# Four slots from the small table instead of three in a mixture-of-experts stage

## The chip, the core and the metric

The program runs on one NeuronCore of a Trainium2 chip, as one launch. Its engines run side by side, each on its own list of instructions: PE (TensorE, matrix products), DVE (VectorE), ACT (ScalarE), POOL (GpSimd) and SP (SyncE, which here only issues transfers). A transfer issued on SP's queue or POOL's queue is carried out by the core's 16 DMA engines. The metric is the time of one execution in microseconds (us). Three runs of the kernel before took 600.97, 602.80 and 606.39 us; the median is 602.8 us.

## What is computed

The input is `x`, 8 batches of 512 tokens of 256 numbers. A first half (an adaptive layer norm, a projection, a short convolution, a 16-state scan and a projection back) is added to `x` under a gate per batch. The second half is a mixture of eight experts, of which each token uses the best one:

```python
h = _layernorm(x, axis=-1) * (1 + cb) + sb
x = x + gb * _L0_ffn_ref(h, ...)

logits = x @ wr + br                      # 8 experts
top_p, top_i = top_k(softmax(logits), 2)
gate = top_p[:, 0] / (top_p[:, 0] + top_p[:, 1])
for e in range(8):                        # only where top_i[:, 0] == e
    hmid = gelu(x @ w1[e] + b1[e])        # 256 -> 1024
    hout = hmid @ w2[e] + b2[e]           # 1024 -> 256
    out += where(top1 == e, hout * gate, 0)
```

All numbers are 32-bit floats. How many tokens an expert gets is known only when the program runs.

## The kernel before, in words

**Stage one** goes through the eight batches. For every token it writes a row of 1028 numbers (4112 bytes) to `xp_d` in DRAM: the result of the first half, its norm and gate, and the batch's three modulation vectors. The token's number is scattered into `ids_d`, a list in DRAM with a region per expert, by four transfers of POOL's queue per batch (`ids_d<-tok,row`).

**Stage two** works in slots. A slot is up to 256 tokens of one expert. It needs the numbers of its tokens (`name_tokens`, line 1023: SP loads a register from a table, then issues `ids<-ids_d`, 1 KB), its expert's weights (`expert_of`, line 1035: SP loads a register, then issues `w1t`, 1 MB, line 1041; `b1t`, line 1044; `b2t`, line 1045; and `w2t`, 1 MB, line 1048), and the rows of its tokens (`rows_of`, line 1055: two transfers of POOL's queue of 128 rows each, `xg<-xp_d,ids`). DVE makes `hg` from `xg`, PE transposes it (`tp<-ident,hg`) and multiplies it with `w1t` (`layer1`, line 1083: eight blocks `ph`, 32 matmuls); ACT applies gelu; PE multiplies with `w2t` (`layer2`, line 1259: two blocks `py`, 32 matmuls); DVE finishes, and POOL scatters the rows to the output (`out<-ot,ids`).

Which expert and which tokens a slot has comes from one of two tables. The **small table** (`early_table`, line 958) is made after six of the eight batches: it holds the first `NEARLY` full groups of 256 tokens. Their rows may be gathered before stage one ends. The **late table** is made after the last batch, and its slots can be named only when the last four `ids_d` scatters have landed. It has `NPAIR = 16 - NEARLY` slots of two tiles and seven of one tile, of which four are always worked on; the other three stand behind a branch (line 1323) that the profiled execution did not take. So 20 slots are worked on: `NEARLY` early ones, then the late ones in the order that lines 1249 to 1255 write out.

```python
got = [slot0, fetched(1, pre[1])] + [fetched(i) for i in range(2, NEARLY)]   # line 1165
...
name_tokens(slots[NEARLY])                                                   # line 1317
work(slots, got, (slot0, gl0, hTs[1]))
```

`fetched` (line 1150) asks for a slot's weights and, unless they are given, its rows. `work` (line 1289) names and fetches slots ahead of the one at hand. Slots 0 and 1 get their rows in stage one (`pre`), slot 0 its weights and first layer too. The weights of the other slots go round four buffers (`wts`), their rows round five.

**The order** in which instructions stand on each engine is not the order in which they are written. All of this is recorded, and a planner (`Plan.order`, line 191) sorts it: it gives each operation an estimated length, takes the operation that can start first by its own clock, and among equals the one that is due first. It counts the transfers of one stage as one wire at 300 GB/s. What it puts out is fixed; on the chip each engine then runs its list in order, and an instruction that waits holds up all that stand behind it. That holds for SP too, whose list is register loads and transfers. The compiled program gives the transfers of SP eight completion lanes in turn, and a transfer waits until the one eight places before it has landed.

Below, slots are called 0, 1, 2 and so on in the order of work; slot 3 is the first late slot before the change, slot 4 after it.

Of the kernel before, what the change touches and what calls it, by code (L numbers as in the profile page):

```python
# [10 lines left out]
FP = mybir.dt.float32  # L11
# [7 lines left out]
P = 128  # L19
# [270 lines left out]
def adaln_mamba_moe_kernel(  # L290
# [16 lines left out]
    B, L, D = x.shape  # L307
# [6 lines left out]
    KF = FF // P  # L314
# [4 lines left out]
    JB = BLK // P  # L319


    FEW, NEARLY = 6, 3
    assert (FEW * NT - E) // 2 + 1 >= NEARLY


# [91 lines left out]
    ids = epool.tile([P, NEARLY + NSLOT, JB], I32, name="ids")  # L417
# [13 lines left out]
    with tc.tile_pool(name="wa", bufs=1) as wa, tc.tile_pool(  # L431
        name="a3", bufs=3
    ) as a3, tc.tile_pool(
        name="a2", bufs=2
    ) as a2, tc.tile_pool(
        name="rowp", bufs=2
    ) as rowp, tc.tile_pool(
        name="sm", bufs=4
    ) as sm, tc.tile_pool(name="ps_t", bufs=2, space=PSUM) as ps_t, tc.tile_pool(
        name="ps_x", bufs=3, space=PSUM  # L440
    ) as ps_x, tc.tile_pool(name="ps_s", bufs=1, space=PSUM) as ps_s, tc.tile_pool(
        name="ps_o", bufs=2, space=PSUM
# [570 lines left out]
        def tiles(i):  # L1013
            return JB if i < NEARLY + NPAIR else 1

        def loads(fn, outs, ins, length):

            if nc is plan:
                plan.call("sync", fn, outs, ins, length)
            else:  # L1020
                fn()

        def name_tokens(i):
            jb, at_ = tiles(i), where[i][1]

            def fn():
                o = chip.sync.value_load(at_, min_val=0, max_val=E * TOK)  # L1027
                chip.sync.dma_start(  # L1028
                    out=ids[:, i, 0:jb],
                    in_=ids_d[bass.ds(o, jb * P), :].rearrange("(p j) o -> p (j o)", j=jb),  # L1030
                )

            loads(fn, [ids[:, i, 0:jb]], [at_, *id_views[: FEW * NT]], 0.8)

        def expert_of(i, w1t, w2t, b1t, b2t, behind=()):

            number = where[i][0]

            def fn():
                e = chip.sync.value_load(number, min_val=0, max_val=E - 1)  # L1040
                chip.sync.dma_start(  # L1041
                    out=w1t, in_=w1[bass.ds(e, 1)].rearrange("o (k p) f -> p (o k) f", p=P)
                )
                chip.sync.dma_start(out=b1t, in_=par[:, bass.ds(e * KF, KF)])
                chip.sync.dma_start(
                    out=b2t, in_=b2[bass.ds(e, 1)].rearrange("o d -> (o d)").partition_broadcast(P)
                )
                chip.sync.dma_start(
                    out=w2t, in_=w2[bass.ds(e, 1)].rearrange("o (k p) d -> p (o k) d", p=P)
                )  # L1050

            loads(fn, [w1t, b1t, b2t, w2t], [number, *behind], 2.5)
            return i, w1t, b1t, b2t, w2t

        def rows_of(i, xg, upto):

            for j in range(tiles(i)):
                nc.gpsimd.indirect_dma_start(
                    out=xg[:, j, :], out_offset=None, in_=xp_d[0:upto, :],
                    in_offset=bass.IndirectOffsetOnAxis(ap=ids[:, i, j : j + 1], axis=0),  # L1060
                    bounds_check=upto - 1, oob_is_err=False,
                )
            return xg
# [19 lines left out]
        def layer1(t, hT, gl, ph_tile):  # L1083
            i, w1t, b1t, b2t, w2t, xg = t
            n = tiles(i) * P
            for f in range(KF):
                ph = ph_tile()
                for k in range(KD):
                    nc.tensor.matmul(
                        ph[:, 0:n], lhsT=w1t[:, k, f * P : (f + 1) * P], rhs=hT[:, k, 0:n],  # L1090
                        start=(k == 0), stop=(k == KD - 1),
                    )
                nc.scalar.activation(gl[:, f, 0:n], ph[:, 0:n], AF.Gelu, bias=b1t[:, f : f + 1])
            return gl
# [4 lines left out]
        for b in range(B):  # L1099
# [6 lines left out]
            if b == FEW - 1:  # L1106
# [5 lines left out]
                pre, hTs = [], []  # L1112
                for i in range(2):
# [13 lines left out]
                slot0 = (*expert_of(  # L1127
                    0, *weights, epool.tile([P, KF], FP, name="b1_0"),
                    epool.tile([P, D], FP, name="b2_0"), pre,
                ), pre[0])  # L1130
# [7 lines left out]
    with tc.tile_pool(name="g", bufs=2) as gp, tc.tile_pool(  # L1138
        name="wts", bufs=4
    ) as wts, tc.tile_pool(name="tab", bufs=1) as tab, tc.tile_pool(  # L1140
        name="blk", bufs=6
    ) as blk, tc.tile_pool(name="blk2", bufs=2) as blk2, tc.tile_pool(name="ps_r", bufs=2, space=PSUM) as ps_r, tc.tile_pool(
        name="ps_h", bufs=4, space=PSUM
# [3 lines left out]
        nc.due = behind + 4 * SLOT  # L1147
        turn = count_from()

        def fetched(i, xg=None):  # L1150
            t = expert_of(
                i, wts.tile([P, KD, FF], FP, name="w1t"), wts.tile([P, KF, D], FP, name="w2t"),
                blk.tile([P, KF], FP, name="b1t"), blk.tile([P, D], FP, name="b2t"),
            )
            if xg is None:

                at = next(turn) % 5
                pool, n = (blk, 3) if at < 3 else (blk2, 2)
                xg = rows_of(
                    i, pool.tile([P, JB, ROW], FP, name="xg", tag=f"xg_{n}", bufs=n),  # L1160
                    FEW * L if i < NEARLY else TOK + BLK,
                )
            return (*t, xg)

        got = [slot0, fetched(1, pre[1])] + [fetched(i) for i in range(2, NEARLY)]


        half = tab.tile([1, 2 * E], I32, name="half")
# [90 lines left out]
        def layer2(t, gl):  # L1259

            i, w1t, b1t, b2t, w2t, xg = t
            mg = xg[:, :, OWN:ROW]
            ot = gp.tile([P, JB, D], FP, name="ot")
            for j in range(tiles(i)):
                py = ps_y.tile([P, D], FP, name="py")
                for f in range(KF):
                    nc.tensor.matmul(
                        py, lhsT=gl[:, f, j * P : (j + 1) * P], rhs=w2t[:, f, :],
                        start=(f == 0), stop=(f == KF - 1),
                    )  # L1270
                nc.vector.tensor_tensor(ot[:, j, :], py, b2t, ALU.add)
                nc.vector.tensor_tensor(ot[:, j, :], ot[:, j, :], mg[:, j, 2 * D : 3 * D], ALU.mult)
                nc.vector.scalar_tensor_tensor(
                    ot[:, j, :], ot[:, j, :], xg[:, j, D + 2 : D + 3], xg[:, j, 0:D],
                    ALU.mult, ALU.add,
                )
                nc.gpsimd.indirect_dma_start(
                    out=outf[i * JB + j],
                    out_offset=bass.IndirectOffsetOnAxis(ap=ids[:, i, j : j + 1], axis=0),
                    in_=ot[:, j, :], in_offset=None, bounds_check=TOK - 1, oob_is_err=False,  # L1280
                )

        def made(t):
            return features(
                t[0], t[-1], gp.tile([P, JB, D], FP, name="hg"),
                gp.tile([P, KD, BLK], FP, name="hT"), ps_r.tile([P, KD, BLK], FP, name="tp"),
            )

        def work(slots, got, begun=None):


            ahead, pending = len(got), None
            hT = None if begun else made(got[0])
            for n in range(len(slots)):
                nc.due = behind + (n + 1) * SLOT
                if n + ahead + 1 < len(slots):
                    name_tokens(slots[n + ahead + 1])
                if n + ahead < len(slots):
                    got.append(fetched(slots[n + ahead]))
                if n == 0 and begun:  # L1300
                    nxt = begun[2]
                else:
                    nxt = made(got[n + 1]) if n + 1 < len(slots) else None
                if n == 0 and begun:
                    layer2(*begun[:2])
                else:
                    gl = layer1(
                        got[n], hT, gp.tile([P, KF, BLK], FP, name="gl"),
                        lambda: ps_h.tile([P, BLK], FP, name="ph"),
                    )  # L1310
                    if pending is not None:
                        layer2(*pending)
                    pending = (got[n], gl)
                hT = nxt
            layer2(*pending)

        name_tokens(slots[NEARLY])
        work(slots, got, (slot0, gl0, hTs[1]))
        plan.emit()
        nc = chip  # L1320
        more = nc.values_load(filled[0:1, 0:1], min_val=0, max_val=NSING)
        for at, part in ((FIRST, rest[:1]), (FIRST + 1, rest[1:])):
            with tc.If(more > at):
                for i in part:
                    name_tokens(i)
                work(part, [fetched(i) for i in part])
# [56 lines left out]
```

## Time and profile before

| what | value |
|---|---|
| median of three runs | 602.8 us (600.97 to 606.39) |
| the profiled execution | 602.82 us, of which 601.0 us from the first to the last instruction (the span) |
| mean granted PE clock | 0.968 of full speed |
| PE busy | 563.9 us, 94% of the span, 2882 matmuls |
| DVE, ACT, POOL busy | 58%, 35%, 35% |
| DMA | 96.73 MB, mean 161 GB/s |
| stage two on PE | from about 321 us (`py` of slot 0) to 587 us |

Times inside the execution are counted in us from its first instruction. In a row of the timeline the columns are the start, the duration, the engine and the source line, the operation with its output and inputs, the number of instructions merged into the row, and in brackets how long the engine was idle before, and what ended it. Most operations are issued through one recording helper, so that nearly all rows name lines 154 and 159; the tile names tell them apart. In a row of a stretch the columns are its bounds, its length, the busy time of each engine with the number of its instructions, the granted PE clock, the busy share of the DMA engines, and what they moved. A chain row is a piece of the chain of work that ended last: start, duration, what. "SPq" is SP's queue of transfers: there the duration of a row includes the time in which the transfer could not be issued.

### The profile page before, as it was taken

How to read it: one execution, taken by the hardware profiler on the slowest of the kernel's cores; microseconds unless marked ns; L12 is line 12 of the kernel's file. 1: busy time of each engine (PE TensorE's matmuls, PEld its weight loads, DVE VectorE, ACT ScalarE, POOL GpSimd, SP SyncE). 2: the span in 40 equal slices, each digit the busy share in tenths (PEclk: the TensorE clock that was granted, in tenths of full speed). 3: DMA queues.
4: the chain of work that ended last, by engine and by line, in shares of the span. 5: the costliest groups of instructions: out<-in, count | busy, mean ns of one | idle time of the engine just before them, and what ended most of it. 6: DMA issues, size and time to landing. Idle time of an engine off the chain costs nothing. (4 is left out here: it accounts for less than half of the span.)

```text
span 601.0 us, 8691 instructions
## 1 busy us (share of the span) xinstructions
PE 563.9 (94%) x2882; PEld 430.1 (72%) x2882; DVE 351.4 (58%) x1087; ACT 210.5 (35%) x404; POOL 209.3 (35%) x334
## 2 busy tenths in 40 slices
PE   5999999999999999999999938999999999999990
PEld 2454766677675766767678826889888988988980
DVE  4879978987878786784876516325234343532210
ACT  2328544544553634432512210223221422222320
POOL 1513663736254453530424142233223322231110
PEclk9779999999999999999999977999999999999996
DMA  7359999410200001010829996999977977972000
GB/s 276 119 148 196 273 254 238 63 51 14 85 1 18 20 1 37 0 37 1 256 72 254 171 342 225 298 382 331 332 245 237 299 252 244 305 245 71 26 3 16
DMA packets 58703, 96.73 MB, mean 161 GB/s; under 512 B 9852, under 2 KB 41854, under 8 KB 58656
## 3 DMA queue, kind: packets, MB, share of 16 engines
q1 hardware_dynamic: 50720, 72.98, 41.2%
q0 software_dynamic: 7936, 23.17, 11.4%
q8 instruction: 24, 0.39, 0.3%
q14 instruction: 23, 0.19, 0.2%
HBM read 86.42 MB, written 22.81 MB: 182 GB/s over the span
## 5 line engine op out<-in xcount | busy, mean ns | idle before, releaser
L159 ACT ACTIVATE gl<-ph,b1t 128x256 f32<-128x256 f32 (+1 forms) x152 | 68.5, 452 | 186.8 <-PE ph L154 180.7
L154 PE MATMUL py<-w2t,gl 128*128 128x256 f32 x476 | 109.8, 383 | 0.0
L154 PEld LDWEIGHTS py<-w2t,gl 128*128 128x128 f32 x476 | 91.7, 193 | 12.9
L159 POOL DMA_INDIRECT out<-ot,ids x36 | 37.7, 1047 | 159.7 <-DVE ot L159 148.6
L159 DVE SCALAR_TENSOR_TENSOR sv<-u,pt,sv 128x512 f32<-128x512 f32 x96 | 77.2, 809 | 12.7 <-ACT sv L159 12.4
L159 PE MATMUL ph<-hT,w1t 128*128 128x256 f32 (+1 forms) x304 | 84.3, 359 | 0.0
L154 PE MATMUL ph<-hT,w1t 128*128 128x256 f32 (+1 forms) x304 | 84.2, 359 | 0.0
L159 DVE TENSOR_TENSOR ot<-py,b2t 128x256 f32<-128x256 f32 x34 | 14.4, 425 | 109.3 <-PE py L154 105.4
L159 PE MATMUL px<-xnT,wi 128*128 128x512 f32 x128 | 69.6, 626 | 0.0
L154 PE MATMUL px<-xnT,wi 128*128 128x512 f32 x128 | 65.9, 597 | 0.0
L154 PEld LDWEIGHTS ph<-hT,w1t 128*128 128x128 f32 x304 | 55.6, 191 | 6.3
L159 PEld LDWEIGHTS ph<-hT,w1t 128*128 128x128 f32 x304 | 55.0, 191 | 6.2 <-issue 0.4
L159 POOL DMA_INDIRECT xg<-xp_d,ids x36 | 37.8, 1051 | 60.9 <-DMA ids<-ids_d 40.5
L159 POOL DMA_INDIRECT ids_d<-tok,row x32 | 34.8, 1087 | 36.1 <-DVE row L159 13.7
L154 PEld LDWEIGHTS px<-xnT,wi 128*128 128x128 f32 x128 | 24.6, 192 | 31.2 <-issue 31.2
L159 ACT COPY u<-px 128x512 f32<-128x512 f32 x32 | 18.7, 585 | 62.6 <-PE px L154 62.1
L159 DVE COPY hT<-tp 128x512 f32<-128x512 f32 (+1 forms) x20 | 12.7, 634 | 36.3 <-PE tp L154 28.1
L159 PEld LDWEIGHTS px<-xnT,wi 128*128 128x128 f32 x128 | 21.3, 192 | 16.4 <-issue 14.8
L159 POOL TENSOR_TENSOR rs<-ve,nhalf 128x4 f32<-128x4 f32 x16 | 19.5, 1219 | 38.7 <-DVE ve L159 29.0
L159 ACT ACTIVATE tz<-px 128x512 f32<-128x512 f32 x32 | 19.1, 595 | 39.3 <-PE px L154 35.7
L159 DVE TENSOR_TENSOR hg<-hg,xg 128x256 f32<-128x256 f32 x72 | 28.9, 422 | 1.2
L159 DVE TENSOR_TENSOR xr<-po,h 128x256 f32<-128x256 f32 x32 | 13.5, 421 | 25.6 <-PE po L154 25.3
(347 smaller groups left out, 947.2 us busy)
## 6 DMA issues: line engine op xcount, KB each, us to landing
w1t<-in_w SPq DMA_DIRECT2D x19, 1024.0 KB
w2t<-in_w SPq DMA_DIRECT2D x19, 1024.0 KB
xp_d<-modb_d SPq DMA_DIRECT2D x8, 1536.0 KB
xp_d<-xr SPq DMA_DIRECT2D x8, 520.0 KB
xt<-in_x SPq DMA_DIRECT2D x8, 512.0 KB
bc<-mod_d SPq DMA_DIRECT2D x7, 384.0 KB
b2t<-in_b SPq DMA_DIRECT2D x19, 128.0 KB
w<-in_w SPq DMA_DIRECT2D x2, 1024.0 KB
```

Of the source, the lines that this page charges most:

```text
L154: me["calls"].append(lambda: getattr(getattr(self.nc, name), op)(*args, **kw))
L159: calls=[lambda: getattr(getattr(self.nc, name), op)(*args, **kw)],
```

## The change

`NEARLY` becomes 4, so the small table names four slots and the late table has twelve pairs instead of thirteen. All tables and lists that are sized by it follow: `sl_at` has 19 columns instead of 20 (four single-element fills on POOL less), the late table's DVE operations 19 columns instead of 20, the small table's four instead of three. `name_tokens` for slot 3 moves to the others of the small table.

`fetched` gets a parameter `after`, handed on to `expert_of` as `behind`: it is a list of tiles that the planner takes as inputs of the weights' load. The load of the new slot 3 is asked for after the first late slot has been named, with that slot's ids as such an input. Nothing on the chip waits for those ids on this account; it is the planner's order alone that they bear on.

```diff
-    FEW, NEARLY = 6, 3
+    FEW, NEARLY = 6, 4
...
-        def fetched(i, xg=None):
+        def fetched(i, xg=None, after=()):
             t = expert_of(
                 i, wts.tile([P, KD, FF], FP, name="w1t"), wts.tile([P, KF, D], FP, name="w2t"),
-                blk.tile([P, KF], FP, name="b1t"), blk.tile([P, D], FP, name="b2t"),
+                blk.tile([P, KF], FP, name="b1t"), blk.tile([P, D], FP, name="b2t"), after,
             )
...
-        got = [slot0, fetched(1, pre[1])] + [fetched(i) for i in range(2, NEARLY)]
+        got = [slot0, fetched(1, pre[1])] + [fetched(i) for i in range(2, NEARLY - 1)]
...
         name_tokens(slots[NEARLY])
+        got.append(fetched(NEARLY - 1, None, [ids[:, NEARLY, :]]))
         work(slots, got, (slot0, gl0, hTs[1]))
```

## The prediction

> **What bounds the kernel now.** First the page: busy PE and granted clock by slices of 15.0 us.
>
> ```profile
> PE   5999999999999999999999938999999999999990
> PEclk9779999999999999999999977999999999999996
> ```
>
> PE is the bound, but for the start and the two slices from 345 to 375 us, which show 3 and 8 tenths and a lower clock. The waits of PE name who it waits for there:
>
> ```profile
> PE tp L159 <- DVE hg L159: 12.2, 4, 9.6
> ```
>
> Its timeline shows the hole: the last row before it, the row that ends it, and the last transposes of slot 4, from which PE runs without a gap until it has finished.
>
> ```profile
> 348.54 0.59 PE L154 MATMUL ph<-hT,w1t 128*128 128x256 f32 x2
> 358.71 0.48 PE L159 MATMUL tp<-ident,hg 128*128 128x128 f32 x1 [9.57 <-DVE hg L159]
> ...
> 373.12 0.27 PE L154 MATMUL tp<-ident,hg 128*128 128x128 f32 x1
> ```
>
> From 349.1 to 373.2 us PE does one block `ph` of slot 2 (two rows 0.43 apart, 0.87 us), eight transposes (0.11 each, 0.9) and `layer2` of slot 2 (two `py` of 3.45, 6.9 us): 8.7 us of work in 24.1. So **15.4 us** are lost, 9.57 + 0.36 + 1.55 in waits for `hg`, the rest to the clock:
>
> ```profile
> 354.00:358.70 4.70, 0.00 (x0) 0.00 (x0) 1.26 (x3) 0.00 (x0) 0.83 (x1) 0.55 1.03 406
> 358.70:364.00 5.30, 3.38 (x10) 2.11 (x11) 3.01 (x7) 0.47 (x1) 2.55 (x3) 0.50 1.05 398
> 364.00:368.00 4.00, 4.00 (x11) 3.20 (x10) 1.75 (x5) 0.00 (x0) 0.00 (x0) 0.50 0.91 316
> ```
>
> The granted clock, the third number from the end, stands at half until 368, 9.3 us after PE resumed. Why `hg` is late, the chain that ended last tells:
>
> ```profile
> 326.25 15.44 DMA ids_d<-tok,row
> 341.93 0.33 SPq L1028
> ```
>
> The last scatters of token numbers, issued from 322.28 to 326.25, land at 341.8, in line with the weights of slots 1 and 2 and the last `xp_d<-xr`. Only then can slot 3's numbers be read (341.93); POOL issues its gathers at 346.60 and 347.96; their rows of 4112 bytes stand in the trace's transfer records at 351.9 to 357.0, behind slot 3's own weights (issued 344.14 and 346.15); DVE starts `hg` at 357.32 and 360.04.
>
> **The change, part by part.** The work is the same: 20 slots, 16 of two tiles and 4 of one, with the same end (one tile, then two). Costs in 285 to 350 us and behind it:
>
> *Slot 3 from the small table.* Its `ids` load is one more at 281 us (three took 3.08 us); behind it on SP stand `xp_d<-xr`, which went at 292.76 anyway, and slot 0's weights: nothing. Its two gathers (1.0 us each) stand in POOL's new order before the last four scatters. POOL was idle for 4.30 us there, until 322.28, and two issues with a gap of 0.3 take 2.4: no cost on POOL. Its `hg` and transposes only move.
>
> *What its 1.05 MB do to the scatters.* They now come first in POOL's own queue and on engines at 0.9 busy. Slot 2's gathers occupied 316.1 to 320.5, 4.4 us alone; beside weights the engines moved 400 GB/s, against 285 alone. So the landing at 341.8 moves by at least 0; by 2.6 if the 1.05 MB go at 400 GB/s; by 9 us if they cost what a megabyte costs at 111 GB/s, the rate at 330 to 336 us. I take **2.6**, the rate of the nearest mixture: call the landing T, 344.4. Slot 2's `w1t` had landed at 340.9 for a use at 342.85; 2.6 us later it costs PE some 1 us, which the hole swallows.
>
> *The hole under the new orders.* PE's new list is: `layer1` of slot 2 (to 350.0), four transposes of slot 4 (now the first late slot), **one block `ph` of slot 3**, then `layer2` of slot 2. The ready `layer2` thus stands behind slot 3's `w1t`. And SP's new list has, after slot 4's ids, **eleven more ids loads** ahead of the weights of slot 3. The planner's wire is full of the weights of slots 1 and 2, so by its clock the ids land late, the load that takes them as input is not ready, and the other ids loads, which are, go first. So the weights are behind twelve ids loads, not one. The price of one, unhindered:
>
> ```profile
> 363.82 11.67 SPq L1028 DMA_DIRECT2D ids<-ids_d  x11
> ```
>
> (11.67 - 0.33) / 10 = 1.13 us. Twelve, and the register load ahead of the weights, take about 13.4 us. So `w1t` of slot 3 is issued at T + 13.4 = 357.8, against 344.14 for the first late slot's before. Its rows took 4.4 us from the issue when nothing stood ahead (slot 3: 344.14 to 348.5; slot 5: 376.65 to 381.1), 12.6 when gathers mixed in (slot 4: 348.60 to 361.2), and what waits for a landing goes on about 2 to 3 us after the last row (357.0 to 360.04 for the second half of slot 3's rows). Ahead of it stand the gathers of slot 4, slot 5 and half of one more, 2.6 MB issued from T + 4.5 on: 9.2 us at 285 GB/s, to about T + 14.7. Bounds from issue to use: 6.4 (4.4 + 2) and 14.6 (12.6 + 2). I take 7.1, near the lower, as the gathers are nearly through. PE goes on at X = 357.8 + 7.1 = **364.9**. The transposes of slot 4 are long done: numbers at T + 4.5, gathers, 6.2 us for rows as in slot 2's case (314.36 to 320.5), landing and `hg`: T + 14 or so.
>
> *From X.* One `ph` (0.87) and `layer2` (6.9) are 7.8 us. The half clock lasts to 368 as before if PE's work from X counts as busy, some 3.1 us at half speed, 1.6 lost: end at 374.3. If it goes on for one more such stretch (6.8 us, half of the 13.6 us seen), 3.4 are lost in all, or 5.0: 376 to 378. I take 2.4 lost: 375.1. By then 0.87 us more work is done than at 373.2 before. Net: 375.1 - 0.87 - 373.2 = **+1.0 us**.
>
> Here a rule of the Trainium skill bears on the clock term: "TensorE: Matmul & The Clock Gate", section "What's actually happening", has the full clock return after one busy window of about 3.4 us; by that the loss is at least 1.7 and the sum +0.3; the row above, half clock for 9.3 us of resumed work, speaks for more.
>
> *Behind it.* Weights of slots 4 and 5 follow slot 3's on SP, four ids loads between. At 300 GB/s slot 4's `w1t` is there by about 373 for a use at 381, slot 5's by 383 for a use at 395. From there four buffers pace the loads as before (SP waited for `ph` and `py` of PE): nothing. If that cover went, each us of lateness is a us of the end.
>
> *Stage one.* Four 1x1 fills less; but the planner's order of the first batches changes on PE, DVE and POOL. PE waits there sum to about 11 us, and two stretches of half clock (20 to 27 and 33 to 40 us). One such stretch more or less is 3.4 us, the bound on either side. I take 0.
>
> Sum: 602.82 + 1.0 = 603.8, that is **604 us**; the profiled execution equals the median of 602.8.
>
> **The rivals.**
>
> *The hole closes* (faster). For it: slot 3's rows are early, and if the scatters are not delayed (T = 341.8) and `w1t` takes 6.4, X is 361.6; with the half clock to 368 the end is 372.6 and the net -1.5 (601.3). If the clock were to stay full it is 369.4 and -4.7; with 3.4 gained in stage one, -8. Against it: PE would idle over 10 us, and a 9.57 us hole was enough for the clock. Below 597 only with both: 596.
>
> *Slot 3's weights arrive last* (slower). The mechanism is the same wait, with T and the transfer at their upper ends: T = 341.8 + 5, issue 360.2, 12 us to use: X = 372.2. End with 2.4 lost 382.4, net +8.3: 611. It decides from X = 370 on (net +6). For it: slot 2's `w1t` took 16.6 us from issue to last row, slot 4's 12.6. Against it: both had 2 MB or more ahead or beside them; here the weights of slots 1 and 2 are done.
>
> *The prefetch runs dry afterwards* (slower): slot 5 misses its weights by a few us and PE stops again; 4 us and a half clock of 3 more make 611. Against it: 12 us of slack above.
>
> **How the numbers follow.** Forecast (a new wait of the same size, 598 to 609): 0.74. Hole closes: 0.07. Weights last: 0.15. Dry: 0.04. A measurement here can tell about 1% (6 us) from nothing; its three runs span 5.4 us. Faster by more than that 0.06, within 0.73, slower 0.21. The range leaves out the lower rival's end and the outer half of the slower ones: 598 to 610.
>
> **What would show it.** After: PE's longest wait at about 350 to 365 us, for `w1t` (a transfer), not for `hg`; SP's row of ids loads x12 from about 344, and `w1t` behind it at about 358; slot 3's gathers on POOL at about 318; the clock at half around 355 to 368 or 375; no PE gap afterwards. Wrong if the scatters land much later than 347, if PE's `tp` of slot 4 is what ends the hole, or if PE in stage one differs by more than 3 us.

## The result, and the profile after

The changed kernel takes 602.27 us (median of 20 runs, 600.30 to 605.29), the kernel before 601.95 us beside it (20 runs): a ratio of 1.0001, 95% interval 0.998 to 1.0021. The forecast was 604 with a range of 598 to 610 and "within 1%" as the likeliest case. The profiled execution has a span of 601.3 us (before: 601.0).

A sum of zero hides large parts. On the page of the changed kernel PE's dip begins one slice of 15 us earlier, is shallower and spreads over three slices instead of two; the clock is down in one of the two slices (360 to 375 us) instead of both:

```profile
PE   5999999999999999999999677999999999999990
PEclk9779999999999999999999997999999999999996
```

PE's timeline from 318 to 400 us has these waits and no other:

```profile
329.06 0.67 PE L159 MATMUL ph<-hT,w1t 128*128 128x256 f32 x2 [0.72 <-DMA w1t<-in_w]
335.75 0.70 PE L159 MATMUL ph<-hT,w1t 128*128 128x256 f32 x2 [3.00 <-ACT gl L159]
341.86 0.70 PE L159 MATMUL py<-w2t,gl 128*128 128x256 f32 x2 [1.73 <-DMA w2t<-in_w]
358.40 0.33 PE L159 MATMUL tp<-ident,hg 128*128 128x128 f32 x1 [2.02 <-DVE hg L159]
365.22 1.19 PE L159 MATMUL ph<-hT,w1t 128*128 128x256 f32 x2 [6.38 <-DMA w1t<-in_w]
...
371.53 3.19 PE L154 MATMUL py<-w2t,gl 128*128 128x256 f32 x14
```

The last row ends `layer2` of slot 2, at 374.7. The old hole was a wait for the rows of the first late slot; the new one is a wait for slot 3's weights, and three smaller waits, for slot 1's weights, stand ahead of it. The chain that ended last says why the weights are late. Its rows are start, duration, what; between the two `SPq` rows stand eleven more pairs of a register load and an ids load:

```profile
325.98 15.67 DMA ids_d<-tok,row
341.85 0.33 SPq L1028
...
354.67 0.28 SPq L1040
355.43 9.65 DMA w1t<-in_w
365.22 1.19 PE ph L159 x2
```

The two holes compare so. Before, 15.4 us were lost between 349.1 and 373.2 us. After, `layer1` of slot 2 ends at 356.0, and from there to 374.7 is a stretch of 18.7 us, with four transposes (0.4), one block `ph` (0.9) and `layer2` (6.9) of work, 8.2 in all: 10.5 us lost. The waits ahead of it are 0.72 + 3.00 + 1.73 = 5.45. Together 15.9, half a us more than before. That half is also the difference of the profiles: from the first `py` of slot 0 to the last instruction the kernel before takes 601.0 - 321.39 = 279.6 us, the changed one 601.3 - 321.17 = 280.1.

### The profile page after: what moved, and what is told of

It is laid out like the page before. It is cut to its first block, busy times and chain, and to the rows that moved or that the text cites. A ratio compares the mean times of both kernels' runs of the same rounds, so it can differ in the third digit from the quotient of the medians.

```text
span 601.3 us, 8671 instructions
## 1 busy us (share of the span) xinstructions
PE 562.8 (94%) x2882; PEld 429.4 (71%) x2882; DVE 348.2 (58%) x1087; ACT 210.8 (35%) x404; POOL 209.6 (35%) x330
## 4 chain that ended last, share of the span: by engine, by line
PE 60%; issue 15%; DMA 14%; POOL 4%; DVE 3%; SPq 2%; ACT 0%; POOLq 0%; ACTq 0%
PE px L159 10%; PE po L154 9%; PE px L154 9%; DMA out<-ot,ids 8%; PE py L154 5%; PE pc L154 3%; PE ph L159 3%; PE ph L154 3%; PE po L159 3%; POOL out L159 3%; PE pd L154 3%; DMA w1t<-in_w 3%; DMA ids_d<-tok,row 3%; POOL xg L159 1%; DVE sv L159 1%
## 5 line engine op out<-in xcount | busy, mean ns | idle before, releaser
L154 PE MATMUL py<-w2t,gl 128*128 128x256 f32 x476 | 108.4, 379 | 0.0
L159 POOL DMA_INDIRECT out<-ot,ids x36 | 36.4, 1011 | 133.9 <-DVE ot L159 101.1
L159 DVE TENSOR_TENSOR ot<-py,b2t 128x256 f32<-128x256 f32 x34 | 14.4, 424 | 117.0 <-PE py L154 117.0
L159 DVE SCALAR_TENSOR_TENSOR sv<-u,pt,sv 128x512 f32<-128x512 f32 x96 | 71.9, 760 | 4.7 <-ACT sv L159 4.7
L159 ACT COPY u<-px 128x512 f32<-128x512 f32 x32 | 18.7, 585 | 67.9 <-PE px L154 67.9
L159 ACT ACTIVATE tz<-px 128x512 f32<-128x512 f32 x32 | 19.0, 595 | 52.0 <-PE px L154 51.8
```

The lines of the kernel that those rows point to most:

```text
L154: me["calls"].append(lambda: getattr(getattr(self.nc, name), op)(*args, **kw))
L159: calls=[lambda: getattr(getattr(self.nc, name), op)(*args, **kw)],
```

## The experiments

All eight are built from the changed kernel, do its whole computation, and are compared with the kernel before. **W** is the stretch of the profiled execution from the first `py` of slot 0 to the last instruction. It leaves out stage one, where runs of any one kernel differ by several us (last section), but it is of one execution each; the medians are of several, stage one included. Each ratio is to 13 or 14 runs of the kernel before made beside that kernel (20 for the changed one), and not to the 601.95 of the first row. **T** is when SP can issue the first ids load of a late slot, since the last `ids_d` scatter has landed.

| kernel | median us (runs) | ratio to before, 95% | W, us |
|---|---|---|---|
| before | 601.95 (20) | | 279.6 |
| after | 602.27 (20) | 1.0001 (0.998 to 1.0021) | 280.1 |
| weights behind one ids load | 599.02 (10) | 0.9948 (0.9907 to 0.9989) | 275.6 |
| weights at once | 592.89 (4) | 0.9835 (0.9778 to 0.9893) | 270.4 |
| `layer2` of slot 2 first | 595.61 (5) | 0.9867 (0.9833 to 0.99) | 274.6 |
| ids loads doubled | 626.8 (1) | | 303.6 |
| slot 2's weights late too | 594.71 (4) | 0.9894 (0.9844 to 0.9944) | 269.2 |
| weights at once, gathers late | 595.46 (5) | 0.9891 (0.9844 to 0.9938) | 271.1 |
| gathers late | 604.81 (10) | 1.0066 (1.0031 to 1.0101) | 281.2 |
| three together | 591.70 (4) | 0.9822 (0.9782 to 0.9862) | 269.1 |

### The weights directly behind slot 4's ids

The planner is told that the load may start as soon as the ids load has been issued, and that it then goes first. On SP this takes eleven ids loads out from ahead of it.

```diff
             for j in o["after"]:
                 a = ops[j]
-                start[j] = max(start[j], end + ...)
+                if a.get("soon") == o["i"]:
+                    start[j], a["due"] = max(start[j], at), -1e9
+                else:
+                    start[j] = max(start[j], end + ...)
...
+        named = len(plan.ops) - 1
         got.append(fetched(NEARLY - 1, None, [ids[:, NEARLY, :]]))
+        plan.ops[named + 1]["soon"] = named
```

> The changed kernel, with slot 3's weights put on SP's list directly behind the ids load of slot 4, so behind one ids load and not twelve. Theory A (the hole ends when slot 3's w1t has landed, and that is late because eleven more ids loads of 1.09 us stand ahead of it; next in line is the first late slot's own rows): w1t is issued at about 343 instead of 355.4, PE no longer waits for it, but slot 4's gathers now stand behind 2 MB of weights as slot 3's did before the change; the wait of PE becomes tp<-hg, the hole ends at about 363 instead of 365.2, total 599 to 601 us, 1 to 3 us under the changed kernel. Theory B (the DMA engines are the limit and the order does not matter): same hole, 602. Theory C (the ids loads are all that is in the way): the hole closes, 592.

Measured: 599.02 us, W 4.5 us less than after. SP's timeline of this kernel:

```profile
342.40 0.33 SPq L1031 DMA_DIRECT2D ids<-ids_d  x1
343.52 0.38 SPq L1044 DMA_DIRECT2D w1t<-in_w  x1
```

and PE's, the two waits of the hole:

```profile
358.49 0.30 PE L159 MATMUL tp<-ident,hg 128*128 128x128 f32 x1 [3.36 <-DVE hg L159]
360.65 0.47 PE L159 MATMUL tp<-ident,hg 128*128 128x128 f32 x1 [1.65 <-DVE hg L159]
```

The weights go 1.1 us after T instead of 13.6, and no wait for them is left. The hole doesn't close: what is late next are slot 4's own rows, as they were for the first late slot before. They now lie behind 2 MB of slot 3's weights (rows of `xg` from 353.2 to 358.7 in the transfer records, against 351.3 to 355.7 after). So the list of ids loads is the bound of the changed kernel, but by this edit alone no more than 4.5 us of W were had.

### The weights of slot 3 at once

The list of inputs is left out; the load follows slot 2's.

```diff
-        got.append(fetched(NEARLY - 1, None, [ids[:, NEARLY, :]]))
+        got.append(fetched(NEARLY - 1))
```

> The changed kernel without the list of ids as an input of the load: slot 3's weights follow slot 2's on SP's list, ahead of the late ids, and PE's list has two blocks ph of slot 3 and layer2 of slot 2 ahead of the transposes of slot 4. Theory A: w1t of slot 3 is issued at about 332 and has landed before 356; PE has 2 + 7 us of work between layer1 of slot 2 and the first late rows, which may then come at 364; the hole of 9 us and its half clock close, total about 592 (590 to 596). Theory B (DMA is the limit): the ids and rows of slot 4 are late by what the weights take, a hole of the same size stands at tp of slot 4, 602.

Measured: 592.89 us, W 270.4. PE has no wait between 341 and 390 us (49.00 us busy of 49.00). The planner, for which slot 3's weights now are early, puts two blocks `ph` of slot 3 and `layer2` of slot 2 ahead of slot 4's transposes. What is left is one wait, for slot 1's transfers:

```profile
332.58 1.19 PE L159 MATMUL ph<-hT,w1t 128*128 128x256 f32 x2 [3.79 <-DMA b2t<-in_b]
```

The ids of slot 4 are read later here (345.07, behind the issue of the weights), and it costs nothing. So a fourth slot from the small table is worth 9 us; the input added to its load, by the orders on SP and PE that the planner makes of it, takes them away again.

### `layer2` of slot 2 ahead of slot 3 on PE

`layer1` of slot 3 is told to wait, in the planner alone, for the last output tile of `layer2` of slot 2. The planner also puts two transposes of slot 5 ahead of that `layer2`.

```diff
+                    first = begun and n == NEARLY - 1
+                    last = layer2(*pending) if first else None
+                    with plan.wanting(done=[last[:, JB - 1, :]] if first else ()):
                         gl = layer1(...)
-                    if pending is not None:
+                    if pending is not None and not first:
                         layer2(*pending)
```

> The changed kernel with PE's list changed alone: layer2 of slot 2 stands ahead of the first block ph of slot 3 (two transposes of slot 5 come before it too). Theory A: w1t is issued and lands as in the changed kernel (355.4, 365), but PE does the 6.9 us of layer2 in that time, from about 360 to 367; gain about 7 us, total 595 (594 to 598). If the time of the hole is set by the clock or by something that comes later, 600 to 602.

Measured: 595.61 us, W 274.6, 5.5 less than after. The profile is of the slowest of the five runs (602.87 us): all of its stage two is about 5 us late, with the first `py` at 326.62. SP's row of twelve ids loads is still there (14.15 us, from 346.40), and `w1t` goes at 362.72. But 6.9 us of ready work now fill the time until it lands, and PE has no wait for it left. What PE waits for ahead of that `layer2` are rows: 1.44 us at 359.48, and

```profile
362.15 0.33 PE L159 MATMUL tp<-ident,hg 128*128 128x128 f32 x1 [2.27 <-DVE hg L159]
364.08 0.45 PE L159 MATMUL tp<-ident,hg 128*128 128x128 f32 x1 [1.48 <-DVE hg L159]
```

The last of these rows are slot 5's, whose transposes the planner put ahead. By W the order on PE was worth about as much as the order on SP (5.5 against 4.5 us); by the medians it was worth more (6.7 against 3.3).

### The late ids loads doubled

Each `ids` load of a late slot but the first is issued twice, register load and transfer, so 23 stand ahead of the weights instead of 12.

> The changed kernel with every late ids load but slot 4's issued twice, so that 23 instead of 12 loads stand ahead of slot 3's weights. Theory A: w1t is issued at 355.4 + 11 x 1.09 = 367.4, PE goes on at 374 to 377 instead of 365.2, total 611 to 616. Theory B (the DMA engines are the limit, not SP's list): under 605.

Measured: 626.8 us, far above the 611 to 616 expected. SP's timeline, the doubled loads and slot 3's weights:

```profile
341.26 41.84 SPq L1029 DMA_DIRECT2D ids<-ids_d  x23
383.89 0.38 SPq L1042 DMA_DIRECT2D w1t<-in_w  x1
```

PE's timeline, the row that ends the hole:

```profile
388.93 1.19 PE L159 MATMUL ph<-hT,w1t 128*128 128x256 f32 x2 [30.17 <-DMA w1t<-in_w]
```

The size was wrong since a load costs 1.82 us here, not 1.1: the second load of a pair writes the same buffer and waits for the first to land. The experiment's point stands: PE goes on 23.7 us later (388.93 against 365.22), and the span is 23.7 us longer (625.0 against 601.3). Behind the hole nothing absorbs the delay. The issue of `w1t` itself came 28.5 us later (383.89 against 355.43); with no gathers beside it and only ids loads ahead of it the transfer took 5.0 us to use instead of 9.8, which gives 4.8 of them back. This kernel was run once; the shift is about twice the widest spread of any kernel's runs here (12.3 us).

### Slot 2's weights behind the ids as well

This asks what T depends on. Slots 2 and 3 both get their weights behind slot 4's ids, in the manner of the first experiment.

```diff
-        got = [slot0, fetched(1, pre[1])] + [fetched(i) for i in range(2, NEARLY - 1)]
+        got = [slot0, fetched(1, pre[1])] + []
...
+        for i in range(2, NEARLY):
+            load = len(plan.ops)
+            got.append(fetched(i, None, [ids[:, NEARLY, :]]))
+            plan.ops[load]["soon"] = named
```

> The changed kernel with the weights of slot 2 as well as slot 3 put on SP's list directly behind the ids load of slot 4. What it tells: why the landing of the last ids_d scatters stayed at 341.85 with a megabyte of gathers more ahead of them. Theory L (transfers are served in the order of issue; in the changed kernel slot 2's weights were issued at 326.95, after the last scatter, and not ahead of it as before): nothing ahead of the scatters changes, they land at 341 to 343, slot 2's w1t is issued at 343 and PE waits some 3 us for it at 349; total about 596 (593 to 599). Theory S (transfers of the two queues share the engines, so slot 2's weights slow the scatters that were issued before them): the landing comes forward to 334 to 338, PE waits nowhere, total about 591.

Measured: 594.71 us, W 269.2. SP's timeline, the first late ids load:

```profile
338.77 0.34 SPq L1031 DMA_DIRECT2D ids<-ids_d  x1
```

PE's timeline from 318 to 400 us, the only wait of over 2 us, for slot 3's `w1t`:

```profile
355.23 0.67 PE L159 MATMUL ph<-hT,w1t 128*128 128x256 f32 x2 [2.34 <-DMA w1t<-in_w]
```

T is 338.77, between the two expectations and nearest to the one by which the scatters share the engines with what is issued after them. From the last scatter's issue to T it is 12.9 us here and 15.9 after (15.0 to 15.4 in three more kernels with the order of after). So 2 MB that were issued from 1 us *behind* the scatters on held them up by 2 to 3 us; the 12.9 is of one execution. And no stretch of half clock is left between 40 and 579 us.

### Slot 3's gathers late, twice

DVE copies slot 3's ids to a tile `late` when the last scatters' numbers are made, and the gathers read that tile: on POOL they then stand behind the scatters. (`fetched` and `rows_of` hand the tile on.) Once in the kernel with the weights at once, once as the only change.

```diff
+        late = tab.tile([P, JB], I32, name="late")
+        with plan.wanting(done=[lim]):
+            nc.vector.tensor_copy(late, ids[:, NEARLY - 1, :])
-        got.append(fetched(NEARLY - 1, None, [ids[:, NEARLY, :]]))
+        got.append(fetched(NEARLY - 1, None, [ids[:, NEARLY, :]], late))
```

> The run without ids as an input of the load (slot 3's weights at once, 592.9) with slot 3's gathers moved behind the last four scatters on POOL (they read a copy of slot 3's ids that DVE makes later). Theory A: the waits of PE for slot 1's loads (3.8 us and a half clock of 6.8 us at 331 to 338) go, but PE then comes some 6 us earlier to the transposes of slot 4 and waits for them there instead: total unchanged, 591 to 594. If the waits for slot 1's loads counted in the end: 586 to 588.

> The changed kernel with slot 3's gathers moved behind the last four scatters on POOL, nothing else. Theory A (PE's waits for slot 1's loads, 0.7 + 3.0 + 1.7 us in the changed kernel, come from these gathers, and are swallowed by the hole, whose end is set from SP's side): the waits go, the hole before slot 3's first block grows by as much, total 602 (600.5 to 604). If they counted in the end: 596 to 597. The landing of the scatters: by theory L at 341 to 343 again, as slot 2's weights come back ahead of them; by a queue of POOL's own, 337 to 338.

Measured, with the weights at once: 595.46 us. Its interval and that of the kernel with early gathers overlap; no gain. The wait of 3.79 us for slot 1 is gone, but slot 3's own rows are late instead, and slot 4's after them, as PE's timeline shows:

```profile
346.25 0.48 PE L159 MATMUL tp<-ident,hg 128*128 128x128 f32 x1 [2.46 <-DVE hg L159]
365.01 0.33 PE L159 MATMUL tp<-ident,hg 128*128 128x128 f32 x1 [1.59 <-DVE hg L159]
```

As the only change: 604.81 us, the expectation that earlier time is swallowed; slower than before by 0.7% even. The waits for slot 1's `w1t` and `b1t` are gone. `w2t` is still waited for (2.58 us), and PE's timeline shows the hole only begin earlier:

```profile
354.78 0.30 PE L159 MATMUL tp<-ident,hg 128*128 128x128 f32 x1 [1.29 <-DVE hg L159]
357.19 0.48 PE L159 MATMUL tp<-ident,hg 128*128 128x128 f32 x1 [2.00 <-issue]
364.61 1.19 PE L159 MATMUL ph<-hT,w1t 128*128 128x256 f32 x2 [6.73 <-DMA w1t<-in_w]
```

PE goes on at 364.61, in a stage that began 0.5 us earlier: no gain. T came 2.4 us earlier, at 339.48, but SP's list then took longer, 16.5 us to the issue of `w1t` (355.94) where it took 13.6 after:

```profile
339.48 14.97 SPq L1028 DMA_DIRECT2D ids<-ids_d  x12
```

Why it took longer was not found out, so how much of the time won an unchanged list would have passed on is open. This hole costs more clock besides: it is at half from 356.5 to 370.2 us, 13.7 in all, where after had 6.8 (361.4 to 368.2), and the same `ph` and `layer2` take 10.8 us instead of 9.5.

### Three together

Weights behind one ids load, gathers behind the scatters, and on PE `layer2` of slot 2, transposes and `ph` of slot 3 ahead of slot 4's transposes.

> An attempt at a faster kernel, from the changed one: slot 3's weights behind one ids load, slot 3's gathers behind the scatters, and layer2 of slot 2 and one block of slot 3 ahead of the transposes of slot 4 on PE. Theory A: PE has 7.8 us of work from 350 on, the transposes of slot 4 can be made at 360 to 361 as in the run with the weights behind one; 3 us of waiting are left: total 590 to 593.

Measured: 591.70 us, ratio 0.9822 (0.9782 to 0.9862). That is faster than the kernel before, as five of the others are; on these few runs it can't be told from the weights at once, whose edit is one line. PE's waits from 318 to 400 us:

```profile
337.44 0.70 PE L159 MATMUL py<-w2t,gl 128*128 128x256 f32 x2 [1.39 <-DMA w2t<-in_w]
347.46 0.44 PE L159 MATMUL tp<-ident,hg 128*128 128x128 f32 x1 [1.99 <-DVE hg L159]
```

## Why the prediction was right, and where only by luck

**The mechanism held.** The likeliest case was "a new wait of the same size", for slot 3's `w1t` behind twelve ids loads. The row on SP was forecast as x12 from about 344, with `w1t` behind it. SP's timeline of the changed kernel:

```profile
341.85 12.78 SPq L1028 DMA_DIRECT2D ids<-ids_d  x12
355.43 0.38 SPq L1041 DMA_DIRECT2D w1t<-in_w  x1
```

The term of 13.4 us for the list is 13.6 (341.85 to 355.43). So close a match is in part luck: in two other kernels the same twelve loads took 16.3 (`layer2` first) and 16.5 us (gathers late) to the issue of `w1t`. Taking the list away took the wait for `w1t` away, and doubling it moved PE's start and the end of the program by the same 23.7 us: the cause is shown, not only argued. X, where PE goes on, was forecast at 364.9 and is 365.2.

**But two terms of X were off, and cancel.** T was forecast to move by 2.6 us, to 344.4; it is 341.85, unmoved. The step that failed is "what its 1.05 MB do to the scatters": it added slot 3's gathers and left all else in place. SP's timeline of the kernel before has this last transfer ahead of slot 2's weights:

```profile
323.01 0.38 SPq L159 DMA_DIRECT2D xp_d<-xr  x1
```

and that of the changed kernel the same transfer and the weights:

```profile
322.77 3.40 SPq L159 DMA_DIRECT2D xp_d<-xr  x1
326.95 0.37 SPq L1041 DMA_DIRECT2D w1t<-in_w  x1
```

Its issue took 3.40 us instead of 0.38, and slot 2's `w1t` went at 326.95 instead of 324.28, now after the last scatter. Slot 2's weights moved behind the scatters as the gathers moved ahead of them. From the last scatter's issue to T it is 15.0 to 15.9 us in the four kernels with both; 12.9 with early gathers and no weights of slot 2; 14.0 and 14.4 with late gathers and the weights ahead (the two such kernels whose ids go first on SP), and 15.7 in the kernel before. So weights behind the scatters are worth 2 to 3 us. The gathers can't be told from the spread of 1.7 us between executions of one order. Early gathers with the weights left ahead, the case for which 2.6 was worked out, were not run: T did not move in the change as it was made, and why not is shown only in part.

The transfer of `w1t` from issue to use was taken at 7.1 us within 6.4 to 14.6; it is 9.8 (355.43 to 365.22). The step said "the gathers are nearly through"; they were not. Rows of `xg` of slots 4, 5 and the single one run from 351.3 to 362.9 in the transfer records, those of `w1t` from 358.5 to 364.3. The undisturbed transfer took 5.0 (ids loads doubled). A T that was put 2.6 us too late and a transfer put 2.7 us too short left X right by chance.

**The clock loss** was taken at 2.4 us and is 1.7: from 365.22 to 374.71 are 9.5 us for 7.8 of work. In the profile of the changed kernel, by stretches (bounds, length, busy time of PE, PEld, DVE, ACT, POOL, granted clock, DMA share, GB/s):

```profile
358.70:364.00 5.30, 0.14 (x2) 0.00 (x0) 2.82 (x8) 0.00 (x0) 0.06 (x1) 0.76 1.00 375
364.00:368.00 4.00, 2.78 (x7) 2.28 (x8) 1.06 (x3) 0.47 (x1) 0.00 (x0) 0.50 1.08 401
368.00:374.70 6.70, 6.70 (x32) 5.91 (x31) 1.33 (x3) 0.00 (x0) 0.99 (x1) 0.98 1.00 337
```

The clock is full again 3.0 us after PE goes on, not 9.3 as before. The row of before was the wrong model: its 9.3 us hold two more waits. The waits are not all of it: the kernel with late gathers has none behind its hole, and the clock was full only 5.6 us after PE went on (364.61 to 370.17). Where PE resumes on the clock's grid counts too (last section).

By the page "TensorE: Matmul & The Clock Gate" of the Trainium skill, section "What's actually happening", the estimate was at least 1.7; the 3.0 us at half clock come to 1.5.

**"Slot 2's `w1t` late costs PE some 1 us"** was wrong in object and size. It was slot 1's `w1t`, `b1t` and `w2t`, and 5.45 us. `b1t` is 4 KB, issued at 319.01; ACT's timeline shows how long it waited for it:

```profile
335.23 2.17 ACT L159 ACTIVATE gl<-ph,b1t 128x256 f32<-128x256 f32 x5 [13.87 <-DMA b1t<-in_par]
```

With the 1.05 MB moved behind the scatters the waits for `w1t` and `b1t` are gone; `w2t` is waited for even then (1.3 to 2.6 us in three kernels); what that part comes from was not tested. That the hole swallows such time fits the kernel with late gathers alone: its hole begins 2.7 us earlier (353.3 against 356.0), and nothing is gained.

**Terms of nothing.** On POOL the scatters begin at 322.05 (before 322.28): the two gathers ahead of them cost nothing. Stage one: the first `py` at 321.17 (before 321.39). Behind the hole PE has no wait to 400 us. All three held, and of the net, +1.0 was forecast and +0.5 is the profile's. Two of the prediction's figures don't come out of its own rows: the lower rival with both its gains is 602.8 - 8 = 594.8, not 596, and the rate at 330 to 336 us is 115 GB/s in the trace, not 111. Neither is in the sum.

**The rivals.** *The hole closes* had a condition (X at 361.6) that did not come about: T was where it asked for, but `w1t` took 9.8 us and not 6.4. What closes the hole is the weights' place on SP ahead of the late ids, as the kernel with the weights at once shows. *Weights last* asked for X from 370 on, by a late T and a long transfer: only the second was there, in part. *The prefetch runs dry* did not happen.

## What to carry to other kernels

An input that exists only in a planner's books still orders a hardware queue: look at what else is ready there, because a dozen cheap transfers of about 1.1 us each can come in ahead of the one that matters. When a dependence on late data is taken away, list the ready work that stands behind the *next* wait on each engine; here one edit of order on SP or on PE was worth 3 to 7 us each, and the slot itself 9. And time won ahead of a wait whose end is set elsewhere was not won here.

## What the runs showed beside this

**When the clock halves.** In all ten traces the clock records change on a grid of 3.41 us: half-clock stretches are 3.4, 6.8, 13.7 or 34.1 us long, but for the last one, which the end of the program cuts. Reading PE's rows from 318 to 400 us against each trace's own grid, the clock halved behind each window in which PE was idle for 58% or more (three together: 1.99 us of 3.41; weights at once, gathers late: 2.4 us; weights at once: 2.3 us), and stayed full behind windows with 57% or less (weights behind one ids load: 1.95 us of its 3.08 us wait; the kernel after: its half-clock stretch begins at 361.40, which puts a bound of the grid at 334.1, so its 3.00 us wait until 335.75 falls into two windows, 1.35 and 1.65). It came back behind a window with 88% busy (after, where PE went on 0.4 us into the window), not behind one with 70% (before) or 63% (gathers late, 1.3 us into it). So a wait of 2.0 us can cost a window at half speed, and one of 3.0 us nothing, by where it falls. The same section of the Trainium skill names one idle window of about 3.4 us as what halves the clock; less was enough here.

Two limits to this. The matmuls' ends are modelled, so the shares are rough, and 57 and 58% are one trace each. And in stage one idle time does not tell it: with the gathers late the clock halved at 35.66 behind a window in which PE was never idle, but mostly did products of 16 columns (`pb`) and of 16 rows (`pq`); in the kernel before it halved at 33.58 behind one with 29%. So the reading is for stage two alone, where nearly all products are 128 rows by 256 columns. What the clock goes by in stage one was not tested.

**Where the spread of one kernel comes from.** In stage one, PE has stretches of half clock at about 20 and 34 us. In most profiled executions the clock is full from 39 to 41 us on, and the first `py` comes at 320.0 to 322.2; in that of `layer2` first it was full only from 51.8 on, and the first `py` came at 326.62, some 5 us later. It was at half clock for 6.8 us more than the changed kernel, which is worth 3.4; and PE waited 3.64 us for DVE at one go (until 30.84), where the changed kernel has two waits of 0.36 and 0.54. Five us is the size of the spread between runs of one kernel. One such execution was caught; that all of the spread is this was not shown.

**An issue that got slower.** The last `xp_d<-xr` took 2.97 to 3.69 us to issue in the six traces with slot 3's gathers ahead of the scatters, and 0.38 in the four others. What it waits for was not found out. Slot 2's weights went behind the scatters with it; whether that is what kept T in place was not tested.
